# A decoder layer with experts on one core: scores from three bfloat16 parts in 64x64 tiles, normalizing on GpSimd, gelus that don't wait for the last exponentials, and first loads ordered by need

## The chip, the core and the metric

The kernel runs on one core of one Trainium2 chip. A core has five engines, each with an instruction queue of its own that it executes in order: TensorE (PE; its weight loads are listed apart as PEld), VectorE (DVE), ScalarE (ACT), GpSimd (POOL) and SyncE (SP). Transfers are issued from the queues of SyncE, ScalarE and GpSimd and carried by 16 DMA engines. Operands lie in SBUF, 128 partitions wide; TensorE writes PSUM, eight banks of 512 float32 a partition. The metric is the device time of one execution in microseconds (us), lower is better. Before has three runs, and one execution was profiled.

## What is computed

One layer of a decoder on x (32, 128, 128) with a context of the same shape; D = 128, 16 heads of 8, 8 experts of 512, two experts a token. All inputs and outputs are float32.

```python
x = layernorm(x + attn(x, x, x, sa_..., causal=True), ln1_g, ln1_b)
x = layernorm(x + attn(x, ctx, ctx, ca_..., causal=False), ln2_g, ln2_b)
x = layernorm(x + moe(x, router_w, router_b, w1, b1, w2, b2), ln3_g, ln3_b)

def attn(...):   # scores = Q K^T / sqrt(8), softmax over keys, times V, times wo, + bo
def moe(x, ...): # softmax of x @ rw + rb, the top 2, softmax of those two;
                 # sum of their experts gelu(x @ w1[e] + b1[e]) @ w2[e] + b2[e]
```

## The kernel before

**Order.** The kernel describes its work as tasks, each with an engine, an estimated duration, a priority, tasks that it depends on and buffers that it holds. `Plan.run` simulates the engines with these durations and fixes one order; `Plan.emit` writes the instructions in that order, so each engine's queue is set by the plan. PSUM is one pool, `s_ps`, of four double banks: a half step of scores takes a double bank, other work single banks. Score tasks have their priority moved ahead by `AHEAD` = 10 steps.

**Items and steps.** The 32 sequences are 8 groups of 4. Each group has a self item ("s") and a cross item ("c"), worked in the order s0 s1 s2 c0 s3 c1 ... s7 c5 c6 c7. A self item has three score tiles (the causal mask removes a quarter): "lo", 0 and 1 for queries and 0, 1 and "hi" for keys; a cross item has four. There are 56 tiles. Each is done twice: once with the queries on the partitions (`scores_q`), from which VectorE takes the negated row maximum (line 963), and `NL` = 3 tiles later with the keys on the partitions (`scores_k`), with the transposed maxima added by matmuls with `sel` (`top_k`), from which ScalarE writes the exponentials `pr` (line 1359). Each tile has two half steps of 8 heads, so 112 half steps each way. `emit_step` merges the query half step of tile i with the key half step of tile i - 3 into one stream: float32 matmuls in 32x64 tiles of the array, the queries on one half of the rows and the keys on the other. Float32 matmuls appear as two instructions. The causal mask is added by matmuls with `idj`.

**Q and K.** `prepare` loads the input, transposes it, projects K and V, and for self items Q (`queries`). Weights are permuted so that four heads' queries can be spread over `qm` by four transfers (line 822), with zeros at other heads' rows:

```python
def masked():
    for r in range(4):
        nc.sync.dma_start(out=it.qm.at[r::4, r, :], in_=it.q.at[r::4, :])
```

**Values and what follows.** `self_values` and `cross_values` multiply `pr` with V and a column of ones; `normalized` transposes on VectorE, takes the reciprocals, multiplies (line 1069) and transposes back; `finish_self` and `cross_out` apply wo and the residual; `norm` is the layer norm (statistics on VectorE, a power on GpSimd, lines 1097 and 1098, scaling on ScalarE). The cross item's Q comes from `finish_self` of its group. `finish_cross` computes the routing (one exponential at line 1212, one at 1290), scatters each token's row twice to its expert's region `rows_d` with eight indirect transfers on GpSimd (line 1266), and writes x2 = normalized * g2 + b2 to SBUF on GpSimd (lines 1186 and 1187).

**Experts.** 71 blocks of 128 rows. Tables (`table`) tell each block's expert; the first 25 blocks need only five groups' routing, the rest all of it and eight fills (line 1560). A block loads its rows and w1 (SyncE), transposes (1606), multiplies by w1 (1624), takes gelu (1633), multiplies by w2 held in `wall` (1641), adds b2 (1654) and scatters its results on GpSimd (1659). Blocks start behind the last score step; a gelu depends on all exponentials:

```python
t = add("ACT", 1.2, pr0 + 0.5, gelu, [t, t_tab, t_b1c, *exps_all], [p1, h])
```

`final` loads a group's results, adds them to x2, normalizes, scales on GpSimd and stores.

**Start.** Weights, biases and constants are loaded by `load`, most of them in ScalarE's queue (line 474); the group inputs by SyncE.

Of the kernel before, what the change touches and what calls it, by code (L numbers as in the profile page):

```python
# [16 lines left out]
P = 128  # L17
H = 16
HD = 8
E = 8  # L20
# [19 lines left out]
CLOCK = 1.0  # L40

# [109 lines left out]
class Plan:  # L151
# [18 lines left out]
    def run(self):  # L170
# [7 lines left out]
        mode = None  # L178
        order, events, k = [], [], 0
# [6 lines left out]
        while left:  # L186
            for e in engines:
                while free[e] <= now + 1e-9 and ready[e]:
                    put, got = [], None
                    while ready[e]:  # L190
                        item = heapq.heappop(ready[e])
                        taken = []
                        ok = True
                        for b in item[2].bufs:
# [24 lines left out]
                    if t.mode is not None:  # L219
# [17 lines left out]
            if what is not None:  # L237
# [15 lines left out]
                else:  # L253
                    heapq.heappush(ready[t.eng], (t.prio, t.start, t))
# [36 lines left out]
def kernel(  # L291
# [66 lines left out]
    idj = sb([P, 2, HALF], "idj", BF16)  # L358
    sel = sb([P, 4, HALF], "sel", BF16)
    maskq = sb([P, 2, HALF], "maskq", BF16)  # L360
    maskk = sb([P, 2, HALF], "maskk", BF16)
# [32 lines left out]
    def c_rowi2():  # L394
        nc.vector.tensor_scalar(ti[:, 1:2], ti[:, 0:1], 31, None, ALU.bitwise_and)
        nc.vector.tensor_copy(rowi, ti[:, 1:2])
# [22 lines left out]
    def c_cols2():  # L419
# [4 lines left out]
        nc.vector.tensor_tensor(tf[:, 128:192], c, r, ALU.subtract)  # L424
        nc.vector.tensor_scalar(tf[:, 192:256], tf[:, 128:192], -32.0, None, ALU.add)
        d = tf[:, 128:256].rearrange("p (j c) -> p j c", j=2)
        nc.vector.tensor_scalar(idj, d, 0.0, None, ALU.is_equal)
# [5 lines left out]
    def c_sel():  # L433
        for r in range(4):
            nc.vector.tensor_scalar(tf[:, r : r + 1], rowi, float(r), None, ALU.is_equal)
            nc.vector.tensor_scalar(tf[:, 4 + r : 5 + r], rowi, float(4 + r), None, ALU.is_equal)
        nc.vector.tensor_tensor(tf[:, 8:12], tf[:, 0:4], tf[:, 4:8], ALU.add)
        nc.vector.tensor_copy(sel, bc(tf[:, 8:12], 2, HALF))

    t_sel = early("DVE", 2.0, -10, c_sel, [t_rowi])  # L440
# [31 lines left out]
    def load(dst, src, prio, q="ACTQ", deps=()):  # L472
        eng = nc.sync if q == "SP" else nc.scalar
        return add(q, 0.12, prio, lambda: eng.dma_start(out=dst, in_=src), deps, lat=DMA)
# [11 lines left out]
    for i, (n, w) in enumerate(  # L486
        (("wqs", sa_wq), ("wks", sa_wk), ("wvs", sa_wv), ("wkc", ca_wk),
         ("wvc", ca_wv), ("wos", sa_wo), ("wqc", ca_wq), ("woc", ca_wo))
    ):
        raw[n] = spare[:, P * i : P * i + P] if n in ("wqs", "wks", "wkc", "wqc") else sb([P, P], n)  # L490
        t_raw[n] = load(raw[n], w, -30 + i)

    bias4 = sb([4, P], "bias4")
    t_b4 = [
        load(bias4[i : i + 1, :], b.rearrange("(o n) -> o n", o=1), -29.9 + 0.01 * i)
        for i, b in enumerate((sa_bq, sa_bk, ca_bq, ca_bk))
    ]
    cols = {}
    t_col = {}
    for n, src in (("g1", ln1_g), ("b1", ln1_b), ("g2", ln2_g), ("b2", ln2_b), ("bvs", sa_bv), ("bvc", ca_bv)):  # L500
        cols[n] = sb([P, 1], "col_" + n)
        t_col[n] = load(cols[n], colsrc(src), -22)
    rws = {}
    t_row = {}
    for n, src, w in (
# [4 lines left out]
        t_row[n] = load(rws[n], rowsrc(src, w), -18 if n != "bos" else -23)  # L510
    rw = sb([P, E], "rw")
    t_rw = load(rw, router_w, -17)


    def permuted(ap):
        return ap.rearrange("p (g r d) -> p g d r", g=4, r=4)

    def as_gdr(ap):
        return ap.rearrange("p (g d r) -> p g d r", g=4, r=4)

    wp = {}
    t_wp = {}
    for i, n in enumerate(("wqs", "wks", "wkc")):
        wp[n] = sb([P, P], n + "p")
        t_wp[n] = early(
            "DVE", 0.3, -15 + i,
# [1225 lines left out]
```

## Time and profile before

| | |
|---|---|
| runs | 746.95, 738.94 and 747.14 us, median 746.95 |
| profiled execution | 744.84 us, of which the span of the trace is 743.1 |
| busy, us | PE 588.1, PEld 475.0, DVE 341.3, ACT 321.0, POOL 259.5 |
| granted TensorE clock, mean | 0.893 |
| DMA | 52.73 MB in 53012 packets, mean 71 GB/s |
| costliest groups | the row maxima, DVE line 963, 137.1 us; the exponentials, ACT line 1359, 114.4 us; score matmuls of 32x128, line 845, 173.8 us |

Times count from the span's start. A row of the timeline gives start, duration, engine, line, operation, and out<-in with partitions x elements; x16 is a count, and rows close together are merged. A row of a group gives busy us and the mean ns of one, then the idle time of the engine ahead of it and what ended it. In a row of windows each engine's busy us and (instruction count) stand in the order PE, PEld, DVE, ACT, POOL, then the clock granted to TensorE as a share, the busy share of the 16 DMA engines, and GB/s; where only some instructions are asked for, engines that have none are left out. Busy time of overlapping instructions counts once, and a matmul's end is modelled.

### The profile page before, as it was taken

How to read it: one execution, taken by the hardware profiler on the slowest of the kernel's cores; microseconds unless marked ns; L12 is line 12 of the kernel's file. 1: busy time of each engine (PE TensorE's matmuls, PEld its weight loads, DVE VectorE, ACT ScalarE, POOL GpSimd, SP SyncE). 2: the span in 40 equal slices, each digit the busy share in tenths (PEclk: the TensorE clock that was granted, in tenths of full speed). 3: DMA queues.
4: the chain of work that ended last, by engine and by line, in shares of the span. 5: the costliest groups of instructions: out<-in, count | busy, mean ns of one | idle time of the engine just before them, and what ended most of it. 6: DMA issues, size and time to landing. Idle time of an engine off the chain costs nothing.

```text
span 743.1 us, 31241 instructions
## 1 busy us (share of the span) xinstructions
PE 588.1 (79%) x12852; PEld 475.0 (64%) x12852; DVE 341.3 (46%) x1009; ACT 321.0 (43%) x717; POOL 259.5 (35%) x440
## 2 busy tenths in 40 slices
PE   1689888998989998998898847985469996877740
PEld 1367666676767776766677736675459985866740
DVE  4445345464665553665655634464022225523332
ACT  0403245454355254254254312544236664556630
POOL 5000011012162422252422063347744444475552
PEclk9957899999999899899999975998859997879985
DMA  6410011000020010010000003022845474555211
GB/s 154 126 36 19 4 41 36 19 24 25 19 70 15 31 41 28 7 60 16 31 21 6 4 29 89 24 63 79 273 113 168 135 218 141 179 154 174 76 52 42
DMA packets 53012, 52.73 MB, mean 71 GB/s; under 512 B 7759, under 2 KB 39415, under 8 KB 52872
## 3 DMA queue, kind: packets, MB, share of 16 engines
q1 hardware_dynamic: 44976, 40.74, 18.6%
q0 software_dynamic: 4576, 9.00, 3.6%
q8 instruction: 103, 1.69, 1.0%
q10 hardware_dynamic: 3320, 1.00, 0.8%
q14 instruction: 37, 0.30, 0.1%
HBM read 35.36 MB, written 11.61 MB: 63 GB/s over the span
## 4 chain that ended last, share of the span: by engine, by line
PE 62%; issue 10%; ACT 7%; DMA 7%; DVE 6%; POOL 3%; SPq 2%; ACTq 2%; DVEq 1%; POOLq 0%
PE ps L845 35%; PE ps L1624 6%; PE ps L1641 6%; PE ps L740 4%; ACT pr L1359 3%; DVE nm L963 2%; PE ps L1606 2%; ACT k L1633 2%; DMA xT<-rows_d 1%; ACT y L1111 1%; POOL rows_d L1266 1%; PE ps L734 1%; PE ps L781 1%; PE ps L1132 1%; DMA res_d<-o,id 1%
## 5 line engine op out<-in xcount | busy, mean ns | idle before, releaser
L963 DVE TENSOR_REDUCE nm<-ps 128x8 f32<-128x1024 f32 (+1 forms) x112 | 137.1, 1224 | 150.3 <-PE ps L845 139.6
L1359 ACT ACTIVATE pr<-ps 128x1024 f32<-128x1024 f32 x112 | 114.4, 1023 | 182.9 <-PE ps L845 170.5
L845 PE MATMUL ps<-k,qm 32*64 32x128 f32 (+1 forms) x4096 | 173.8, 284 | 7.1 <-DMA qm<-q 5.3
L845 PEld LDWEIGHTS ps<-k,qm 32*64 32x64 f32 x4096 | 133.8, 145 | 35.8 <-issue 27.9
L845 PE MATMUL ps<-qm,k 32*64 32x512 f32 (+1 forms) x1024 | 131.7, 590 | 16.2 <-ACT pr L1359 5.4
L1633 ACT ACTIVATE k<-ps,b1c 128x128 f32<-128x128 f32 x284 | 80.6, 372 | 58.5 <-PE ps L1624 49.6
L975 POOL CAST nmx<-nm 128x16 bf16<-128x16 f32 x64 | 12.9, 201 | 249.2 <-DVE nm L963 242.5
L1641 PE MATMUL ps<-wall,k 128*128 x568 | 82.5, 292 | 17.1 <-ACT k L1633 13.3
L1659 POOL DMA_INDIRECT res_d<-o,id x71 | 69.8, 983 | 60.0 <-DVE o L1654 47.7
L845 PE MATMUL ps<-pr,v 64*32 64x64 f32 (+2 forms) x3072 | 76.0, 271 | 14.2 <-issue 10.1
L1641 PEld LDWEIGHTS ps<-wall,k 128*128 128x128 f32 x568 | 72.3, 200 | 22.0 <-ACT k L1633 15.1
L845 PEld LDWEIGHTS ps<-pr,v 64*32 64x32 f32 (+1 forms) x3072 | 59.2, 112 | 26.1 <-issue 16.3
L1266 POOL DMA_INDIRECT rows_d<-y,rid x64 | 64.2, 1003 | 28.9 <-issue 17.3
L845 PEld LDWEIGHTS ps<-qm,k 32*64 32x64 f32 x1024 | 32.0, 135 | 37.1 <-ACT pr L1359 11.5
L1624 PE MATMUL ps<-bx,qm 128*128 128x128 f32 x368 | 55.5, 301 | 0.0
L1651 DVE TENSOR_SCALAR id<-xT,tab_e 128x1 int32<-128x1 f32 x47 | 12.8, 273 | 89.3 <-PE ps L1606 21.9
L845 PE MATMUL ps<-nmT,sel 32*64 32x128 bf16 x1792 | 52.4, 225 | 1.6 <-issue 1.6
L1624 PEld LDWEIGHTS ps<-bx,qm 128*128 128x128 f32 x368 | 51.3, 216 | 0.4 <-ACT bx L1611 0.3
L1611 ACT ACTIVATE bx<-ps,col_b,col_g 128x128 f32<-128x128 f32 x71 | 32.3, 468 | 30.8 <-PE ps L1606 30.5
L845 PEld LDWEIGHTS <-sel 32*64 32x64 bf16 x1792 | 39.6, 106 | 6.6 <-issue 6.1
L1606 PE MATMUL ps<-ident,xT 128*128 128x128 f32 x47 | 15.0, 319 | 24.2 <-DMA xT<-rows_d 18.6
L1111 ACT ACTIVATE y<-ps,rs 128x128 f32<-128x128 f32 x64 | 24.7, 460 | 16.9 <-DVE rs L1103 16.9
(263 smaller groups left out, 867.8 us busy)
## 6 DMA issues: line engine op xcount, KB each, us to landing
qm<-in_L_xattn_e_w_dram SPq DMA_DIRECT2D x46, 256.0 KB, 3.2
w<-in_L_xattn_e_w_dram SPq DMA_DIRECT2D x25, 256.0 KB, 2.9
qm<-q SPq DMA_DIRECT2D x64, 64.0 KB, 1.9
pr<-res_d SPq DMA_DIRECT2D x8, 512.0 KB
xT<-rows_d SPq DMA_DIRECT2D x47, 65.0 KB, 2.1
xin<-in_x_dram SPq DMA_DIRECT2D x8, 256.0 KB, 3.2
xin<-in_ctx_dram SPq DMA_DIRECT2D x8, 256.0 KB, 4.2
wall<-in_L_xattn_e_w_dram SPq DMA_DIRECT2D x8, 256.0 KB, 5.9
```

Source lines behind the costliest of these rows:

```text
L740: nc.tensor.matmul(bank, lhsT=w, rhs=xT.rearrange("p s t -> p (s t)"), start=True, stop=True)
L845: nc.tensor.matmul(out_, lhsT=lhsT, rhs=rhs, start=start, stop=stop, skip_group_check=True)
L963: lambda: nc.vector.tensor_reduce(dst(), src(), AX.X, ALU.max, negate=True), [dep], [pair, nm],
L1111: lambda i=i: nc.scalar.activation(dst(i), src(i), AF.Identity, bias=rs.at[:, 1, i : i + 1], scale=rs.at[:, 0, i : i + 1],),
L1266: nc.gpsimd.indirect_dma_start(out=rows_d[:, :], out_offset=bass.IndirectOffsetOnAxis(ap=rid.at[:, i, k : k + 1], axis=0), in_=y.at[:, i, ...
L1359: lambda kp=kp, prb=prb, kh=kh: nc.scalar.activation(prb.at[:, 8 * kh : 8 * kh + 8, :].rearrange("p h q -> p (h q)"), kp.at.rearrange("p b ...
L1606: nc.tensor.transpose(bt.at[:, 0:P], xr_()[:, 0:P], ident)
L1611: lambda: nc.scalar.activation(xT.at[:, 0:P], bt.at[:, 0:P], AF.Identity, bias=cols["b2"], scale=cols["g2"]),
L1624: nc.tensor.matmul(p1.at[:, c * P : (c + 1) * P], lhsT=w1.at[:, c, :], rhs=xT.at[:, 0:P], start=True, stop=True)
L1633: nc.scalar.activation(h.at[:, c, :], p1.at[:, c * P : (c + 1) * P], AF.Gelu, bias=b1c[:, bass.ds(r + c, 1)],)
L1641: nc.tensor.matmul(p2.at[:, 0:P], lhsT=h.at[:, c, :], rhs=flat[:, bass.ds(w["pe"] + c * P, P)], start=c == 0, stop=c == NFC - 1,)
L1659: nc.gpsimd.indirect_dma_start(out=res_d[:, :], out_offset=bass.IndirectOffsetOnAxis(ap=idb.at[:, 0:1], axis=0), in_=o.at, in_offset=None, ...
```

## The change

- **Scores.** Q and K are each cut into three bfloat16 parts. The projection is biased and rounded to the first part on ScalarE, the remainder is taken on VectorE, cast to the second part and subtracted to the third on GpSimd. The three go to DRAM in one transfer (`pd`), and six transfers gather them into `qk` [128, 8, 512] so that 64 rows hold one head's 8 dimensions times six products of parts and two rows of zeros. Scores are bfloat16 matmuls in 64x64 tiles, a query and a key task of their own instead of the merged step. At most two query and two key half steps are in flight (`TQ`, `TK`), a query tile waits for the keys of `LOCK` = 2 steps back, keys trail by `NL` = 2 tiles, and the loads of an item wait for the step 4 before it (`LEAD`). Weights are no longer permuted.
- **Normalizing.** The multiply of `normalized` moves from VectorE to GpSimd.
- **Gelus.** They no longer depend on the exponentials; the plan knows which table ScalarE holds and keeps gelus together. The routing's second exponential becomes a tanh in all groups, the first one in the last two.
- **x2** is written to DRAM and loaded again in `final`; the scaling on GpSimd comes behind the row scatters.
- **First loads.** The first input comes first, ScalarE's queue has four loads (wq, wk and their biases of self attention), everything else goes to SyncE by need.
- **Buffers.** Three `k` buffers where four were (only for h now), four `pr` for five, 12 late buffers for h of the rest blocks; estimated durations in the plan are changed.

The core of the diff:

```diff
+TABLE = 1.3
+BURST = 3
...
+                        if e == "ACT" and item[2].mode not in (None, table):
+                            same = any(u.mode == table for _, _, u in ready[e]) or any(u.mode == table for _, _, u in put)
+                            if same or (table == "exp" and exps and gelus < BURST):
+                                put.append(item)
+                                continue
...
-    qm_t = places(3, [P, 4, G * P], "qm")
+    qk_t = places(6, [P, 8, G * P], "qk", BF16)
+    s_p3 = Slots(places(2, [P, 3, G * P], "p3", BF16))
...
-    NL = 3
-    GATE = 4
+    NL = 2
+    LEAD = 4
+    TQ, TK, LOCK = 2, 2, 2
...
+    def parts(w, b, xT, deps, prio, terms, name):
+        bank, p3, r1, at = Buf(s_ps), Buf(s_p3), Buf(s_r1), Buf(s_qk)
+        pd = dram.tile([3, P, G * P], BF16, name="pd_" + name)
+        t1 = pe(1.12, prio, lambda: project(bank.at, w, xT.at), deps, [bank, xT, p3])
+        t2 = add(
             "ACT", act(512, 1), prio + 0.1,
+            lambda: nc.scalar.activation(p3.at[:, 0, :], bank.at, AF.Identity, bias=b), [t1], [bank, p3],
+        )
+        t3 = add(
+            "DVE", dve(512), prio + 0.2,
+            lambda: nc.vector.scalar_tensor_tensor(r1.at, bank.at, b, p3.at[:, 0, :], ALU.add, ALU.subtract),
+            [t2], [bank, p3, r1],
+        )
+        t4 = add("POOL", 0.8, prio + 0.3, lambda: nc.gpsimd.tensor_copy(p3.at[:, 1, :], r1.at), [t3], [p3, r1])
+        t5 = add(
+            "POOL", pool_tt(512), prio + 0.4,
+            lambda: nc.gpsimd.tensor_tensor(p3.at[:, 2, :], r1.at, p3.at[:, 1, :], ALU.subtract), [t4], [p3, r1],
+        )
+        t6 = add(
+            "SP", 0.5, prio + 0.5, lambda: nc.sync.dma_start(out=pd.rearrange("k p n -> p k n"), in_=p3.at), [t5], [p3], lat=2.2
+        )
+
+        def loads():
+            for t, k in enumerate(terms):
+                nc.sync.dma_start(
+                    out=at.at[t::8], in_=pd[k - 1].rearrange("(i a) n -> a i n", i=8)
+                )
+
+        t7 = add("SP", 3.0, prio + 0.6, loads, [t6, *t_qz[0 : 2 if name in ("qs0", "ks0") else 6]], [at], lat=3.0)
+        return at, t7, t5
...
+    def scores_q(sq, h, pair):
...
+        for r in range(4):
+            i = 4 * h + r
+            for n in range(len(cols_[0])):
+                for j in range(2):
+                    rr = slice(HALF * j, HALF * j + HALF)
+                    for ct in range(2):
+                        s, q0, k0, nk, c0 = cols_[ct][n]
+                        mm(pair[HALF * ct : HALF * ct + HALF, j, r * P + c0 : r * P + c0 + nk],
+                           Q[rr, i, s * P + q0 : s * P + q0 + HALF], K[rr, i, s * P + k0 : s * P + k0 + nk],
+                           r == 0 and n == 0, r == 3 and sq[0] == "c" and n == len(cols_[0]) - 1)
...
-            nc.vector.tensor_tensor(
+            nc.gpsimd.tensor_tensor(
                 u2.at.rearrange("p (b a j d) -> p a b j d", a=2, j=2, d=HD),
...
-        t_e = add("ACT", 0.25, prio + 1.1, lambda: nc.scalar.activation(v(96, 32), v(64, 32), AF.Exp), [t1], [rt])
+        late_ = gi >= NG - 2
+        t_e = add(
+            "ACT", 0.25, prio + 1.1,
+            lambda: nc.scalar.activation(v(96, 32), v(64, 32), AF.Tanh if late_ else AF.Exp, scale=0.5 if late_ else 1.0),
+            [t1], [rt], mode=None if late_ else "exp",
+        )
...
+            items[sq[0], sq[1]].t_Q.deps.append(step_tasks[i - LEAD])
+            items[sq[0], sq[1]].t_K.deps.append(step_tasks[i - LEAD])
...
-        t = add("ACT", 1.2, pr0 + 0.5, gelu, [t, t_tab, t_b1c, *exps_all], [p1, h])
+        t = add("ACT", 1.2, pr0 + 0.5, gelu, [t, t_tab, t_b1c], [p1, h], mode="gelu")
...
+        t_y = add(
+            "SP", 0.4, pr0 - 2, lambda: nc.sync.dma_start(out=y.at.rearrange("p s d -> p (s d)"), in_=x2_d[gi]),
+            [items["c", gi].t_x2, *exps_all], [y], lat=2.5,
+        )
```

More of the change, by code (lines that the diff above doesn't have):

```diff
@@ L178, in run @@
         mode = None
+        table, exps, gelus = "exp", sum(t.mode == "exp" for t in self.tasks), 0
         order, events, k = [], [], 0
@@ L218, in run @@
                     d = t.dur
-                    if t.mode is not None:
+                    if e == "ACT":
+                        exps -= t.mode == "exp"
+                        gelus -= t.mode == "gelu"
+                        if t.mode not in (None, table):
+                            table = t.mode
+                            d += TABLE
+                    elif t.mode is not None:
                         if mode is not None and t.mode != mode:
@@ L253, in run @@
                 else:
+                    gelus += t.mode == "gelu"
                     heapq.heappush(ready[t.eng], (t.prio, t.start, t))
@@ L433, in c_sel @@
     def c_sel():
[L434 to L440, printed above, removed]
+        c = tf[:, 64:72]
+        nc.vector.tensor_tensor(tf[:, 0:8], c, rowi.broadcast_to([P, 8]), ALU.is_equal)
+        nc.vector.tensor_scalar(tf[:, 8:16], c, 8.0, None, ALU.add)
+        nc.vector.tensor_tensor(tf[:, 8:16], tf[:, 8:16], rowi.broadcast_to([P, 8]), ALU.is_equal)
+        nc.vector.tensor_tensor(tf[:, 0:8], tf[:, 0:8], tf[:, 8:16], ALU.add)
+        nc.vector.tensor_copy(sel, bc(tf[:, 0:8], 2, HALF))
+    t_sel = early("DVE", 1.2, -10, c_sel, [t_rowi, t_cols])
     def c_misc():
@@ L596 @@
     )
-    x2 = [sb([P, G, P], f"x2_{g_}") for g_ in range(NG)]
-    b1r = sb([E * NFC, P], "b1r")
+    x2_d = [dram.tile([P, G * P], F32, name=f"x2_{g_}") for g_ in range(NG)]
+    b1r = spare[0 : E * NFC, P : 2 * P]
     b1c = sb([P, E * NFC], "b1c")
     b2r = sb([P, E, P], "b2r")
+    t_b1r = load(b1r, e_b1.rearrange("e (c f) -> (e c) f", f=P), 7, "SP")
+    bb = Buf(s_ps)
+    t = pe(0.2, 12, lambda bb=bb: nc.tensor.transpose(bb.at[:, 0 : E * NFC], b1r, ident[: E * NFC, : E * NFC]), [t_b1r, t_ident], [bb], "32x128")
+    t_b1c = add("DVE", 0.2, 12.1, lambda bb=bb: nc.vector.tensor_copy(b1c, bb.at[:, 0 : E * NFC]), [t], [bb])
     t_wall = []
@@ L683 @@
     t_qz = [
-        early("POOL" if i == 1 else "DVE", 1.3 if i != 1 else 1.9, -21 + 9 * i,
-              lambda i=i: (nc.gpsimd if i == 1 else nc.vector).memset(qm_t[i], 0.0))
-        for i in range(3)
-    ]
+        early("POOL" if i % 2 else "DVE", 1.8, -21 + 2 * i,
+              lambda i=i: (nc.gpsimd if i % 2 else nc.vector).memset(qk_t[i].bitcast(F32), 0.0))
+        for i in range(6)
+    ]
+    for q_, t in zip(s_qk.free, t_qz):
+        q_.last = [t]
     t_nz = early("POOL", 0.8, -12, lambda: [nc.gpsimd.memset(n, 0.0) for n in nmx_t])
@@ L943, in emit_step @@
[L943 to L954 removed]
+                        mm(pair[HALF * ct : HALF * ct + HALF, j, r * P + c0 : r * P + c0 + nq],
+                           K[rr, i, s * P + k0 : s * P + k0 + HALF], Q[rr, i, s * P + q0 : s * P + q0 + nq],
+                           r == 0 and n == 0, False)
@@ L1074, in mul @@
             )
-        t = add("DVE", dve(256), prio + 0.02, mul, [t], [u1, rc, u2])
+        t = add("POOL", pool_tt(256), prio + 0.02, mul, [t], [u1, rc, u2])
         t = add(
```

436 lines of the change are left out of this document (180 added, 256 removed).

## The prediction

> **What bounds the kernel now.** I read the busy times first, then the stages, then inside each stage what its first late engine waits for.
>
> ```profile
> PE 588.1 (79%) x12852; PEld 475.0 (64%) x12852; DVE 341.3 (46%) x1009; ACT 321.0 (43%) x717; POOL 259.5 (35%) x440
> ```
>
> TensorE is the busiest engine by far, but 79% is an average. The windows cut the span at the first score (38.7 us) and the last one (484.8 us); the columns are busy us of each engine, then the granted clock and the DMA share.
>
> ```profile
> 38.70:93.00 54.30, 48.33 (x1495) 38.59 (x1501) 23.77 (x32) 13.57 (x20) 4.01 (x20) 0.69 0.05 16
> 93.00:260.00 167.00, 152.22 (x4675) 115.57 (x4659) 92.53 (x210) 76.55 (x126) 40.30 (x94) 0.98 0.10 31
> 260.00:427.30 167.30, 151.03 (x4414) 116.55 (x4412) 96.78 (x246) 75.69 (x127) 46.87 (x107) 0.97 0.08 24
> 427.30:450.40 23.10, 11.79 (x90) 9.03 (x90) 8.13 (x41) 4.88 (x13) 13.28 (x15) 0.72 0.10 34
> 450.40:484.80 34.40, 31.33 (x750) 22.33 (x754) 17.85 (x45) 14.09 (x19) 11.29 (x25) 0.79 0.19 53
> sum 446.10, PE 394.70 PEld 302.07 DVE 239.07 ACT 184.79 POOL 115.75; mean PE 78.94 PEld 60.41 DVE 47.81 ACT 36.96 POOL 23.15
> ```
>
> So the attention stage takes 446.1 us, TensorE works 394.7 of them (91% from 93 to 427 us), and 51.4 are idle, 11.3 of these in the hole at 427 to 450 us. It is a TensorE stage. The next two rows are the same windows summed for line 845 alone (scores and values), and for the tile pr (values only).
>
> ```profile
> sum 446.10, PE 286.36 PEld 222.32; mean PE 57.27 PEld 44.46
> ...
> sum 446.10, PE 73.06 PEld 56.80 DVE 0.00 ACT 113.35; mean PE 14.61 PEld 11.36 DVE 0.00 ACT 22.67
> ```
>
> Scores take 286.4 - 73.1 = 213.3 us of TensorE, 1.90 us for each of 112 half steps. The 181.4 us beside them (394.7 - 213.3) stay. Ahead of this stage ScalarE starts late; behind it the experts' stage has its holes:
>
> ```profile
> 0.79 0.43 ACTq L474 DMA_DIRECT2D wall<-in_L_xattn_sa_wq_dram  x1
> ...
> 17.90 0.33 ACTq L474 DMA_DIRECT2D rw<-in_L_xattn_router_w_dram  x1
> 18.26 1.28 ACT L758 ACT_TABLE_LOAD   x1 [18.26 <-DMA row_g<-in_L_xattn_ln_g_dram]
> ```
> ```profile
> 484.80:508.00 23.20, 15.40 (x196) 13.71 (x193) 13.11 (x72) 10.17 (x24) 12.85 (x18) 0.96 0.26 87
> 508.00:530.00 22.00, 18.65 (x136) 17.17 (x136) 7.09 (x33) 12.36 (x44) 16.36 (x22) 0.89 0.42 121
> 530.00:544.70 14.70, 0.45 (x1) 0.18 (x1) 2.35 (x10) 0.46 (x1) 10.58 (x11) 0.61 0.75 248
> 544.70:613.00 68.30, 65.85 (x485) 60.51 (x485) 13.78 (x57) 43.13 (x144) 28.23 (x30) 0.93 0.58 163
> 613.00:725.00 112.00, 78.21 (x551) 72.12 (x551) 45.09 (x187) 59.76 (x189) 61.49 (x63) 0.86 0.44 129
> ```
>
> From 484.8 to 544.7 us TensorE idles 59.9 - 34.5 = 25.4 us; from 544.7 to 613 it is full.
>
> **The scores.** A half step of queries becomes 16 pairs of a weight load and a bfloat16 matmul (32 where a tile has two halves), one of keys the same, plus 16 pairs for the maxima; a masked half step adds 4 pairs. Over 112 half steps each way: 2048 + 2048 + 1792 + 384 = 6272 pairs, four at a time in the 64x64 tiles. The trace has no 64x64 score, but it has 16 pairs of bfloat16 with 128 columns, four at a time, whose successor begins right behind them:
>
> ```profile
> 480.92 0.40 PE L845 MATMUL ps<-nmT,sel 32*64 32x128 bf16 x16
> 480.92 0.24 PEld L845 LDWEIGHTS <-sel 32*64 32x64 bf16 x12 [0.30 <-issue]
> 481.25 0.30 PEld L1162 LDWEIGHTS ps<-woc,oT 128*128 128x128 f32 x2
> ```
>
> From 480.92 to 481.25 is 0.33 us for 16, or 20.6 ns a pair: 129 us in all. The 384 masks are two to four times as wide (16 us more at three times), 1024 pairs are half as wide (10 us less at half): 135 us. The first tenth runs at the clock of 0.69 seen above, for which I add 10 us: 145. TensorE gains 213 - 145 = 68 us. The bounds: the weight loads alone start every 12 ns or so ((0.24 us less one load of 0.106, a mean from the group below) / 11), which would give 75 us and a gain of 138; and at 34 ns (213.3 / 6272) nothing is gained. I take 20.6 because that row has the new type and width.
>
> ```profile
> L845 PEld LDWEIGHTS <-sel 32*64 32x64 bf16 x1792 | 39.6, 106 | 6.6 <-issue 6.1
> L845 PE MATMUL ps<-nmT,sel 32*64 32x128 bf16 x1792 | 52.4, 225 | 1.6 <-issue 1.6
> ```
>
> A rule speaks against this. The Trainium skill, "TensorEngine Tiling (Array Packing)", section "Key Properties", says that changing the tiling mode drains TensorE. The row just shown has its successor in another mode 0.33 us behind the first start, so one such drain is inside my 20.6 ns; no run here shows the 64x64 mode itself. Splitting each mixed step into a query and a key group makes 112 more boundaries; what they could cost is a rival below.
>
> **What the scores now need first.** Each of 32 projections (16 items, Q and K) is cut into three parts and goes through DRAM. These are the nearest rows:
>
> ```profile
> L771 ACT ACTIVATE k<-ps,bqk 128x512 f32<-128x512 f32 x16 | 11.0, 690 | 23.3 <-PE ps L740 23.3
> 419.39 0.68 DVE L1497 TENSOR_TENSOR u<-ps,key_first 128x512 f32<-128x512 f32 x1
> L1187 POOL TENSOR_TENSOR x<-x,row_b 128x512 f32<-128x512 f32 x8 | 10.2, 1271 | 0.6
> L822 SPq DMA_DIRECT2D qm<-q x64: 458/592/1868, 34.2 to 448.4; - x64
> DMA to landing us min/median/max: 1.8/1.9/3.9
> L1069 DVE TENSOR_TENSOR u<-u,rc 128x256 f32<-128x256 f32 x32 | 13.3, 427 | 0.4
> ```
>
> The ScalarE pass (0.69) stays. New are a VectorE difference of 0.68 us (the row reads PSUM at the same size), a GpSimd cast (no row; I take 0.85, between nothing and the 1.27 of a two-input pass) and a GpSimd difference of 1.27; then one store (0.59 to issue, 1.9 to land) and six loads (3.55, 1.9) where four transfers stood (2.37, 1.9). The way from projection to score grows from 4.3 to 10.7 us, up to 14.7 with both landings at 3.9. By engine: VectorE 239 + 32 x 0.68 - 32 x 0.43 (the multiply that leaves) = 247; GpSimd 116 + 32 x 2.12 + 32 x 0.64 (half of 1.27) = 204; SyncE issues 224 transfers for 132 us. None reaches TensorE's 181 + 145 = 326 us.
>
> The longer way is covered in mid-stage, where a cross item waits behind four other items' steps. It isn't at the end, in the hole from 427 us: there the last cross queries wait for a norm that stands behind eight scatters in GpSimd's queue,
>
> ```profile
> 428.55 1.12 POOL L1266 DMA_INDIRECT rows_d<-y,rid  x1 [1.76 <-DVE whi L1296]
> ...
> 439.18 1.04 POOL L1098 TENSOR_TENSOR rs<-rs,mhalf 128x4 f32<-128x4 f32 x1
> ```
>
> and the 6 to 10 us come on top; I count 8. Elsewhere idle grows because VectorE (247 us) is now close behind, and the split maxima (nmx) and norms wait behind longer GpSimd work. Two new limits, two query and two key groups in flight and queries held until the keys of two steps back are issued, put waits at the head of TensorE's queue, with values and projections behind them. Against that the keys trail by two tiles where they trailed by three. I count 11 more. So idle goes from 51 to 70, bounds 51 and its double. Attention: 326 + 70 = 396, **-50 us** (from -138 to about +50, were nothing gained and idle doubled).
>
> The multiply on GpSimd costs 0.64 for 0.43, 32 times, in chains that scores cover; for the last group it is 0.4 us on the path. TensorE keeps all its other work. The eight wall loads now wait for the transposed b1 too; wall is first read at 508 us. Fewer constants, unpermuted weights and one vector less in the routing are nothing beside these.
>
> **The start.** ScalarE issues 27 loads until 18.2 us and only then loads its table; the first score follows at 38.8.
>
> ```profile
> 0.80 3.44 DMA xin<-in_x_dram
> ...
> 20.99 5.46 PE ps L740 x8
> ...
> 38.81 3.86 PE ps L845 x124
> ```
>
>  Now it issues four (27 from 0.79 to 18.2 are 0.64 us each with their waits, 0.43 for one alone), and SyncE has the rest. After: input landed at 4.3, transposes and copy 6.5, both projections 10.7 (eight pieces took 5.46 with their waits, so four about 2.7 to 4), parts 14, store 17, 12 loads and landing 26; SyncE's own 30 or so loads (13 us at 0.43, 19 at 0.64) can stand ahead of the stores, so I take 28: **-11 us** (from -15 to 0).
>
> **The experts.** Gelus waited for the last routing exponential:
>
> ```profile
> 506.48 1.28 ACT L1633 ACT_TABLE_LOAD   x1 [0.47 <-DVE wlo L1295]
> 507.78 5.26 ACT L1633 ACTIVATE k<-ps,b1c 128x128 f32<-128x128 f32 x20
> 525.06 0.97 POOL L1560 DMA_INDIRECT rows_d<-fillrow,fid  x1 [0.30 <-issue]
> 535.27 0.97 POOL L1659 DMA_INDIRECT res_d<-o,id  x1 [0.30 <-issue]
> ```
>
> Freed, they can start behind the last score's exponential, some 20 us sooner. What is late next is GpSimd: its eight row scatters and eight fills stand ahead of the results' scatters (535.27), and with four result buffers the experts stop. So of 25.4 us idle I take 15: **-15 us**. Bounds: -25, and +8, since eight reloads of x2 join SyncE's queue and three h buffers stand where four did. The tanh in routing costs three VectorE instructions of about 0.17 us, twice, beside other work.
>
> **The sum.** 743.1 - 50 - 11 - 15 = 667.1 us span; the profiled run took 744.84, 1.7 more, so **669 us**. The runs' median is 746.95; 2% of it, 15 us, is what a measurement of this kernel can tell.
>
> **Rivals.**
> 1. *Boundaries* (0.06). Each of 112 new boundaries waits for the last matmul to leave: its 225 ns less the 82 that its tile takes a pair anyway (4 x 20.6), 0.14 us, 16 us: 685. For it: separate groups; against: the row at 481.25. This is what the skill's drain would do.
> 2. *Others pace* (0.14). VectorE's reduce sits in every half step, GpSimd doubles its work; idle doubles to 103 us. Attention 429: 702. For it: 247 us of VectorE in a stage of 396. Against: it waits for TensorE today.
> 3. *The clock falls* (0.06). The windows grant 0.69 to 0.79 where TensorE is broken up and 0.98 where it is 91% busy. With 82% busy it might average 0.75 for 0.91: 326 x 0.91 / 0.75 = 396 + idle 50: 446, so 719. The Trainium skill, "TensorE: Matmul & The Clock Gate", section "What's actually happening", has half rate after an idle window; the windows at 0.69 to 0.79 agree in kind.
> 4. *Slower: the round trip through SyncE* (0.07). An item's loads start four tile steps ahead, and SyncE executes in order, so a store that waits for GpSimd holds up every load behind it. By rows the pair of projections needs 14 x 0.59 + 2 x 1.9 + 4 = 16 us against four steps of 396 / 58 = 27. If small rows of 1 KB made it 37, an item (3.5 steps) would take 32.4: 16 x 32.4 = 518 for 446, so 790. It turns slower than now beyond 34 us. For it: DRAM and 16 partitions a load, no row; against: twice the slack.
> 5. *It does more* (0.10). Idle stays at 51, the hole shrinks, the experts gain all 25: 640 or less.
>
> The forecast keeps 0.57. Also possible: that tanh is not in the same table as exp or gelu, 1.28 us a switch; at most some 10 us in the transition, inside the range. Range: from 615 (rival 5, pairs nearer 15 ns) to 725 (rival 3). Faster by over 2% (below 730): 0.57 + 0.06 + 0.14 + 0.10 and half of 3, **0.90**; within 2% the other half, **0.03**; slower **0.07**.
>
> **What will show it.** Scores: a cross half step of queries near 0.33 us and of keys near 0.66; the stage from first to last score near 396, TensorE near 326 in it, VectorE near 247, GpSimd near 204. First score near 28 us. First gelu within 3 us of the last exponential; TensorE idle in the next 60 us nearer 10 than 25. Wrong if pairs cost 30 ns or more, if score matmuls wait for the loads of the parts, or if the clock in mid-stage is below 0.85.

## The result: 705 us where 669 were forecast, and the profile after

The changed kernel takes 705.23 us (median of four executions), against 743.63 us for the kernel before beside it: a ratio of 0.948, 95% interval [0.940, 0.957]. Three of the four lie between 704.14 and 705.83 us; one, with a granted clock of 0.63, took 745.16 us and is left out of the ratio. The direction was right. The size was not: the span fell by 40.7 us (743.1 to 702.4), where I had summed 76.

The first line of the profile after shows what a reader wants first: TensorE has 81 us less work, and is idle more.

```profile
PE 507.0 (72%) x11443; PEld 407.8 (58%) x11443; DVE 355.2 (51%) x996; ACT 319.3 (45%) x717; POOL 335.1 (48%) x538
```

The windows from the first score (33.8 us) to the last one (448.6 us) of the changed kernel, and then the sums of the same windows for line 845 alone (scores and values) and for the tile pr (values only):

```profile
33.80:93.00 59.20, 43.32 (x1590) 31.32 (x1589) 32.63 (x60) 22.16 (x33) 17.36 (x44) 0.87 0.44 132
93.00:260.00 167.00, 134.11 (x4265) 101.56 (x4267) 106.92 (x225) 83.86 (x140) 75.75 (x146) 0.96 0.42 127
260.00:402.10 142.10, 112.13 (x3627) 88.45 (x3614) 87.02 (x222) 66.37 (x112) 61.81 (x122) 0.94 0.31 96
402.10:422.60 20.50, 11.16 (x131) 9.03 (x124) 8.07 (x32) 5.08 (x9) 15.19 (x18) 0.75 0.31 98
422.60:448.60 26.00, 17.86 (x477) 14.39 (x476) 18.83 (x65) 9.47 (x19) 15.64 (x33) 0.67 0.28 78
sum 414.80, PE 318.59 PEld 244.76 DVE 253.47 ACT 186.94 POOL 185.76; mean PE 63.72 PEld 48.95 DVE 50.69 ACT 37.39 POOL 37.15
```
```profile
sum 414.80, PE 198.58 PEld 157.09; mean PE 39.72 PEld 31.42
...
sum 414.80, PE 71.46 PEld 55.10 DVE 0.00 ACT 108.02; mean PE 14.29 PEld 11.02 DVE 0.00 ACT 21.60
```

So 40.7 us have three sources. The start gave 5 (first score at 33.8 for 38.8). The attention stage gave 31 (446.1 to 414.8). Behind the last score 253.8 us are left for 258.3, which is 4.5. In the stage TensorE's work fell by 76 us (394.7 to 318.6), more than forecast, and its idle time rose by 45 (51.4 to 96.2). The views of TensorE's waits in that stretch say where; the columns are the total, the number of times and the longest one. Before, then after:

```profile
PE ps L845 <- issue: 14.1, 17, 1.7
...
PE ps L1162 <- DVE oT L1079: 1.7, 1, 1.7
```
```profile
PE ps L845 <- issue: 30.3, 25, 2.4
PE ps L1128 <- DVE oT L1045: 19.9, 5, 8.7
PE ps L845 <- DVE nm L923: 7.9, 9, 2.6
```

Two rows make 34 of the 45 us: "issue", a wait for nothing that the profile shows, and the cross output (line 1162 before, 1128 after) waiting for the transposed values. By the windows, the hole before the last cross item didn't grow (9.3 us idle from 402 to 422 us, 11.3 before); idle time grew in the windows around it. Behind the last score, the gelus do start early, as meant (5.0 us behind the last exponential, which ends at 450.4 us), and then something new appears; the rows are ScalarE's timeline, two windows, and TensorE's waits there:

```profile
454.07 1.28 ACT L1622 ACT_TABLE_LOAD   x1 [2.30 <-PE ps L1595]
455.36 1.14 ACT L1622 ACTIVATE k<-ps,b1c 128x128 f32<-128x128 f32 x4
```
```profile
448.60:508.70 60.10, 45.15 (x415) 40.21 (x404) 18.04 (x94) 31.94 (x97) 41.37 (x48) 1.00 0.61 175
508.70:577.00 68.30, 50.08 (x363) 44.69 (x363) 13.36 (x54) 31.74 (x106) 25.23 (x26) 0.90 0.52 154
```
```profile
PE ps L1613 <- ACT qk L1622: 12.9, 22, 0.7
PE ps L1613 <- ACT k L1622: 5.3, 8, 0.8
```

In the first 60 us TensorE idles 15.0 us where before it idled 25.4; but in the next 68 us it idles 18.2, where before it was full (2.5). The first matmul of a block (line 1613) waits 30 times for the gelu of the block ahead of it. One round, from the timeline:

```profile
541.72 1.16 PE L1613 MATMUL ps<-bx,qk 128*128 128x128 f32 x8 [0.66 <-ACT qk L1622]
...
543.35 1.14 ACT L1622 ACTIVATE qk<-ps,b1c 128x128 f32<-128x128 f32 x4 [1.33 <-PE ps L1613]
...
544.54 1.16 PE L1613 MATMUL ps<-bx,qk 128*128 128x128 f32 x8 [0.66 <-ACT qk L1622]
```

A block's first matmuls of 1.16 us, 0.47 until the gelu starts, 1.14 of gelu, and at once the next block's matmuls: a loop of 2.82 us through one PSUM bank. The block's output bank is the one that the previous gelu has just left. In the kernel before, the median distance of two blocks is 2.22 us.

### The profile page after: what moved, and what is told of

Its sections match the earlier page's. It is cut to its first block, busy times and chain, and to the rows that moved or that the text cites. A ratio compares the mean times of both kernels' runs of the same rounds, so it can differ in the third digit from the quotient of the medians.

```text
span 702.4 us, 28754 instructions
## 1 busy us (share of the span) xinstructions
PE 507.0 (72%) x11443; PEld 407.8 (58%) x11443; DVE 355.2 (51%) x996; ACT 319.3 (45%) x717; POOL 335.1 (48%) x538
## 4 chain that ended last, share of the span: by engine, by line
PE 33%; DVE 15%; issue 14%; DMA 11%; POOL 10%; ACT 8%; SPq 6%; ACTq 2%; DVEq 1%; POOLq 0%
PE ps L845 14%; PE ps L1613 6%; DVE nm L923 5%; POOL rows_d L1232 4%; SPq L819 4%; PE ps L1630 3%; ACT pr L1340 2%; ACT qk L1622 2%; DMA pd_qs<-p 2%; DVE y L1678 2%; DMA pr<-res_d 2%; PE ps L733 2%; ACT k L1622 1%; DVE st L1057 1%; DMA qk<-pd_ks 1%
## 5 line engine op out<-in xcount | busy, mean ns | idle before, releaser
L845 PE MATMUL ps<-qk,qk 64*64 64x128 bf16 (+1 forms) x4096 | 98.8, 226 | 27.5 <-DVE nm L923 7.9
L845 PEld LDWEIGHTS <-qk 64*64 64x64 bf16 x4096 | 70.3, 115 | 60.7 <-issue 28.4
L845 PE MATMUL ps<-pr,v 64*32 64x128 f32 (+2 forms) x3072 | 73.6, 265 | 20.4 <-issue 14.2
L1622 ACT ACTIVATE qk<-ps,b1c 128x128 f32<-128x128 f32 x184 | 52.4, 368 | 45.0 <-PE ps L1613 41.8
L1613 PE MATMUL ps<-bx,qk 128*128 128x128 f32 x368 | 54.6, 295 | 17.6 <-ACT qk L1622 12.9
L1613 PEld LDWEIGHTS ps<-bx,qk 128*128 128x128 f32 x368 | 47.7, 203 | 24.0 <-ACT qk L1622 18.2
L845 PE MATMUL ps<-nmT,sel 64*64 64x128 bf16 x1792 | 49.7, 227 | 7.0 <-issue 6.6
L1630 PE MATMUL ps<-wall,qk 128*128 x368 | 50.2, 282 | 5.1 <-ACT qk L1622 2.3
L1630 PEld LDWEIGHTS ps<-wall,qk 128*128 128x128 f32 x368 | 45.4, 195 | 6.7 <-ACT qk L1622 3.3
L1622 ACT ACTIVATE k<-ps,b1c 128x128 f32<-128x128 f32 x100 | 28.6, 369 | 30.7 <-PE ps L1613 23.6
L1600 ACT ACTIVATE bx<-ps,col_b,col_g 128x128 f32<-128x128 f32 x71 | 32.6, 470 | 20.6 <-PE ps L1595 19.7
```

Of the source, the lines that this page charges most:

```text
L845: nc.tensor.matmul(out_, lhsT=lhsT, rhs=rhs, start=start, stop=stop, skip_group_check=True)
L1600: lambda: nc.scalar.activation(xT.at[:, 0:P], bt.at[:, 0:P], AF.Identity, bias=cols["b2"], scale=cols["g2"]),
L1613: nc.tensor.matmul(p1.at[:, c * P : (c + 1) * P], lhsT=w1.at[:, c, :], rhs=xT.at[:, 0:P], start=True, stop=True)
L1622: nc.scalar.activation(h.at[:, c, :], p1.at[:, c * P : (c + 1) * P], AF.Gelu, bias=b1c[:, bass.ds(r + c, 1)],)
L1630: nc.tensor.matmul(p2.at[:, 0:P], lhsT=h.at[:, c, :], rhs=flat[:, bass.ds(w["pe"] + c * P, P)], start=c == 0, stop=c == NFC - 1,)
```

## The experiments

They ran on three other chips, on which the kernel before takes 824 to 830 us with a clock of about 0.85; so ratios are compared, or times on these chips, which differ by some us for one kernel. The times expected below were reckoned for the first chip; run again on one of these, the changed kernel itself has a ratio of 0.933, not 0.948, and its edits have to be set against that. My theory after the comparison: **(a)** the gelus earned their 15 us, and the planner's new durations took them back through the reuse of a bank; **(b)** in attention "issue" is TensorE waiting for its own instructions; **(c)** the cross output waits because the multiply stands in GpSimd's queue. The rivals: VectorE and GpSimd pace the stage, as in the prediction's second rival, and what follows the gelus sets the end anyway.

**Banks.** For the experts' blocks the planner takes the half bank given back longest ago:

```diff
+        if n == 0:
+            free = [(self.given.get((i, h), 0), -i, h) for i, u in enumerate(self.used) for h in range(2) if not u[h]]
...
+            _, i, h = min(free)
```

> The changed kernel with one edit in the planner: the experts' blocks take the PSUM half bank that was given back longest ago, not the one given back last. Theory (bank reuse): the new estimated durations let the plan give the next block's first matmul the bank that the previous block's gelu has just left, so TensorE waits for ScalarE's gelu in 30 blocks, 18.2 us in all (12.9 + 5.3). With other banks these waits fall below 4 us, the pitch of a block in the long stretch from 2.82 to about 2.2 us, and the kernel takes 705 - 15 = 690 us (684 to 697). Rival (the gelu's own chain paces the blocks: 0.47 us to start, 1.14 to run, then the copy of the next rows): the waits get another name, the pitch stays at 2.8 us, and the time stays within 3 us of 705.

Measured: 750.14 us, ratio 0.907 [0.899, 0.916]. TensorE no longer waits for a gelu at the first matmul, and the median distance of blocks is 2.27 us. Its second matmuls in the long stretch come 2.0 us apart:

```profile
599.95 1.07 PE L1640 MATMUL ps<-wall,qk 128*128 x8
602.07 1.06 PE L1640 MATMUL ps<-wall,qk 128*128 x8
603.97 1.09 PE L1640 MATMUL ps<-wall,qk 128*128 x8
```

Theory (a) holds: from the last score to the end are 266.4 us. It is also the fastest version of this study that computes the whole layer. Run again on another chip:

> The kernel with the experts' banks given in turn once more, as the measure for the two beside it. Theory: ratio to the kernel before 0.907 as measured (0.895 to 0.92), 264 to 268 us behind the last score. Rival (the first reading was a disturbed one): 0.93 or more.

Measured: 751.73 us, ratio 0.913 [0.903, 0.922], 266.0 us behind the last score. The changed kernel itself, for comparison:

> The changed kernel as it is, as the measure for the edits run beside it on the same chip, since chips differ in their granted clock. Theory (the gelus earned their 15 us and the reuse of a PSUM bank took them back): its ratio to the kernel before is 0.948, as measured first, equal to that of the gated kernel (0.949) within 0.012 only if gating also hides the reuse; I expect 0.93 to 0.95, its stage from first to last score on a chip of the same clock within 5 us of those of the three edits before (445 to 449 us), and the time behind the last score within 5 us of the 284.7 us of the kernel with the multiply on VectorE. Rival (the rotation of banks did something else): the time behind the last score is below 275 us here too.

Measured: 770.2 us, ratio 0.933 [0.923, 0.943]; 280.1 us behind the last score, 4.6 less than the kernel with the multiply on VectorE, as the theory had it. The stage took 455.8 us, 7 to 11 more than the edits before it, so it missed that part; kernels with one order of instructions differ by up to 10 us in this stage from chip to chip. Behind the last score the banks are worth 14 us against this kernel.

**Gating.** The gelus wait for all exponentials and the routing again; the edit also takes them out of the planner's rule about tables:

```diff
-        t = add("ACT", 1.2, pr0 + 0.5, gelu, [t, t_tab, t_b1c], [p1, h], mode="gelu")
+        t = add("ACT", 1.2, pr0 + 0.5, gelu, [t, t_tab, t_b1c, *exps_all], [p1, h])
+        exps_all.append(t_e2)
```

> The changed kernel with the gelus waiting again for the last score exponential and for the routing's second function of all groups (which stays a tanh), without the planner's table rule. This undoes the part that the prediction put at -15 us. If freeing the gelus is worth that, this kernel takes 720 us (714 to 728), with the first gelu some 25 us behind the last exponential instead of 5. Rival (what follows, GpSimd's scatters and the fills, sets the experts' end either way): 703 to 709.

Measured: 782.27 us, ratio 0.949 [0.942, 0.956]. The last score is at 478.2 us, and ScalarE loads the gelu's table 34 us later:

```profile
512.27 1.28 ACT L1623 ACT_TABLE_LOAD   x1 [0.46 <-DVE rt L1220]
513.57 3.20 ACT L1623 ACTIVATE k<-ps,b1c 128x128 f32<-128x128 f32 x12
```

Behind the last score 300.3 us are left, 16 to 20 more than in the two ungated kernels with the old banks (284.7 and 280.1). And with both edits:

> Both edits together: banks given in turn, and the gelus gated again by the exponentials and the routing. It completes the square of gating and banks. Theory (two separate effects, gelus freed 15 us, banks 16 to 18): the time behind the last score is that of the kernel with the banks alone plus 15 us (280 to 286), ratio about 0.927. Rival (the reuse of banks matters only because the gelus are spread; gated gelus run in bursts in another order): gating costs less than 5 us here.

Measured: 765.23 us, ratio 0.922 [0.910, 0.933]; 280.9 us behind the last score, 15 more than the banks alone. The square is complete: freeing the gelus is worth 15 to 20 us whichever banks are used, the reuse of banks costs 14 to 19 whether they are gated or not. The rival falls.

**The multiply.** Back on VectorE:

```diff
-            nc.gpsimd.tensor_tensor(
+            nc.vector.tensor_tensor(
...
-        t = add("POOL", pool_tt(256), prio + 0.02, mul, [t], [u1, rc, u2])
+        t = add("DVE", dve(256), prio + 0.02, mul, [t], [u1, rc, u2])
```

> The changed kernel with the multiply of the normalizing put back on VectorE. Theory (a queue behind GpSimd): TensorE's waits of the cross output for the transposed values (21.4 us in all, 8.7 of them in the hole at 407 us) come from the multiply standing in GpSimd's queue behind scatters, casts and the maxima's split; they fall below 9 us and the kernel takes 694 us (687 to 701). Rival (VectorE paces the stage, as in the prediction's second rival): 32 multiplies of 0.43 us more on VectorE make the maxima later; the wait for the output shrinks but TensorE waits longer for the maxima, and the time is 703 to 712.

Measured: 769.54 us, ratio 0.936 [0.927, 0.944]. That would be the theory's 694 us on the first chip, but the changed kernel itself has 0.933 on such a chip, so nothing is gained. The wait of the cross output falls from 6.6 us (in the banks' kernel on the same chip) to 1.9, and the stage doesn't shorten. Its window, and that of the banks' kernel on the same chip:

```profile
33.20:481.60 448.40, 342.49 (x10054) 255.08 (x10057) 255.89 (x608) 185.69 (x308) 167.78 (x324) 0.84 0.34 105
```
```profile
33.10:480.60 447.50, 339.99 (x10048) 254.43 (x10047) 250.39 (x602) 187.26 (x310) 186.17 (x361) 0.87 0.34 105
```

So the multiply has no price on this chip, but only one such wait stood there, 6.6 us in the hole. On the first chip there were five, 19.9 us, and its trace shows the queue that theory (c) named. At each of the five the multiply (line 1035) ran behind the group's eight scatters (line 1232), as here:

```profile
295.53 0.35 DVE L1027 RECIPROCAL rc<-u 128x32 f32<-128x32 f32 x1
296.37 0.97 POOL L1232 DMA_INDIRECT rows_d<-y,rid  x1 [0.30 <-issue]
300.97 0.61 POOL L1035 TENSOR_TENSOR u<-u,rc 128x256 f32<-128x256 f32 x1
302.12 0.79 PE L1128 MATMUL ps<-woc,oT 128*128 128x128 f32 x2 [3.27 <-DVE oT L1045]
```

Its operand was there at 295.88 us, the last scatter ended at 297.34, a norm and parts came next, and the multiply started at 300.97. What this costs the stage on the first chip was not measured.

**TensorE or the others?** Two edits that leave every queue's order as it is, and leave out work. One takes 1344 pairs from TensorE, the other 57 us from VectorE:

```diff
-        for r in range(4):
+        for r in (3,):
```

> The changed kernel with the row maxima subtracted for one of each four heads only: 12 of the 16 pairs with sel leave each key half step, 1344 pairs in all, every queue otherwise in the same order. (It leaves out the subtraction for the other heads.) Theory (TensorE with its instruction blocks still sets most of the stage): 1344 pairs at 20.3 ns are 27 us of work, and 10.5 blocks of instructions at 3.5 us or more need not be fetched, so the stalls at blocks (36 us) fall by 8 to 15: the stage shortens by 30 us (24 to 42). Rival (the others pace it, as in the prediction's second rival): the freed time turns into waits for VectorE and GpSimd, and the stage shortens by less than 12 us.

```diff
-            src = lambda: pair.at.rearrange("p b (r k) -> p (b r) k", r=4)
+            src = lambda: pair.at.rearrange("p b (r k) -> p (b r) k", r=4)[:, :, 0:HALF]
```

> The changed kernel with each row maximum taken over the first half of its columns, all queues in the same order. (It leaves out the other half of the columns.) A reduce takes about 0.69 us for 1.22, 59 us less of VectorE's 253 in the stage. Theory (TensorE and its instruction blocks): only the 5 to 8 us of waits for a maximum go, the stage shortens by 3 to 10 us. Rival (VectorE paces the stage, the prediction's second rival): it shortens by 25 us or more.

Measured: 741.32 us, ratio 0.896 [0.885, 0.908], and 762.29 us, ratio 0.926 [0.916, 0.936]. The stage's windows of the unedited kernel, of fewer maxima and of the half reduce, all on one chip:

```profile
34.10:489.90 455.80, 341.10 (x10047) 255.77 (x10047) 249.94 (x601) 186.36 (x308) 185.88 (x360) 0.86 0.34 104
```
```profile
33.40:453.80 420.40, 317.68 (x8704) 230.35 (x8703) 248.67 (x602) 185.51 (x309) 186.49 (x360) 0.86 0.36 111
```
```profile
33.10:474.70 441.60, 336.38 (x10048) 256.74 (x10047) 192.92 (x602) 186.62 (x310) 186.12 (x361) 0.86 0.34 106
```

Fewer pairs shorten the stage by 35.4 us (24 to 42 expected), 12 more than TensorE's busy time falls (23.4); TensorE's idle time falls too. (Set against the same order on the other two chips, 447.5 and 446.4 us, it is 26 to 27.) Taking 57 us from VectorE shortens it by 14.2, or by 5 to 6 when set against the other two chips, somewhere between the bounds of the two theories, but far from 57. TensorE still sets most of this stage, and VectorE a little of it.

**The instructions.** A series of independent pairs with nothing else:

> Not the decoder: only series of independent bfloat16 matmuls in 64x64 tiles of TensorE, four tiles in turn, 1152 pairs of a weight load and a matmul with 64 columns, 1152 with 128, 768 with 256, and again 1152 with 128 beside transfers of the kind that gather the parts. Theory (instruction stream): 16 KB blocks of instructions, 256 instructions or 128 pairs each, arrive no faster than one in 3.4 to 3.7 us, so long series of 64 and of 128 columns both take 27 to 29 ns a pair, with stalls of 1 to 2 us at every block, while 256 columns take about 45 ns without stalls; the transfers change this by less than 10%. Rival (the stalls in the kernel come from the transfers of the parts beside them): 128 columns take 20 to 22 ns a pair without stalls, and only the last series has them. Second rival (the stalls come from waits on other engines that the trace doesn't name): no stalls in any series.

TensorE's timeline in the series of 64 columns and of 128; x128 is the number of matmuls in one burst. Then the windows of the series of 64, 128 and 256 columns, and of 128 beside the transfers:

```profile
13.41 1.92 PE L365 MATMUL n<-wide 64*64 64x64 bf16 x128 [4.74 <-issue]
16.86 1.92 PE L365 MATMUL n<-wide 64*64 64x64 bf16 x128 [1.53 <-issue]
...
45.86 1.98 PE L365 MATMUL n<-wide 64*64 64x128 bf16 x128 [1.47 <-issue]
49.59 1.98 PE L365 MATMUL n<-wide 64*64 64x128 bf16 x128 [1.75 <-issue]
```
```profile
13.41:38.68 25.27, 13.45 (x896) 12.51 (x896) 0.00 (x0) 0.00 (x0) 1.00 0.02 5
45.86:70.87 25.01, 13.87 (x898) 12.85 (x897) 0.00 (x0) 0.00 (x0) 1.00 0.02 5
81.06:96.37 15.31, 15.26 (x546) 14.86 (x548) 0.00 (x0) 0.00 (x0) 1.00 0.02 6
98.88:130.08 31.20, 15.85 (x1024) 14.68 (x1024) 0.00 (x0) 0.00 (x0) 1.00 0.52 162
```

This is the clearest picture of the study. With 64 and 128 columns TensorE runs exactly 128 pairs in 1.92 to 1.98 us, 15 ns a pair, and then stands still until 3.45 to 4 us have passed since the burst began. Sustained, a pair costs 28 ns with 64 columns (25.27 / 896) and with 128 (25.01 / 898). With 256 it costs 28 ns too (15.31 / 546), where I had expected 45; there TensorE is busy all the time, 3.6 us for 128 pairs, and no stall shows. Beside the transfers it is 30.5 (31.20 / 1024), 9% more. The queue for instructions in the decoder's own profile has the size that belongs to it:

```profile
q8 instruction: 92, 1.51, 0.9%
```

That is 16.4 KB a packet, and 2 x 11443 instructions in 92 packets, some 249 in each. The decoder's own traces settle it, for they hold the time of each packet and of each instruction. In the changed kernel all 25 waits of the row "issue" at line 845 end 1.22 to 1.59 us behind the arrival of such a packet, and all stand at one place, give or take one, in a count of TensorE's instructions by 256. So do 16 of the 17 in the kernel before. Theory (b) holds, for the whole of that row on the first chip. It also explains the edit of the maxima: in the unedited kernel beside it 27 waits at this place take 30.2 us, with fewer pairs 13 take 12.6.

**The start**, with the first keys' store and loads in ScalarE's queue, and the banks:

```diff
+        q, eng = ("ACT", nc.scalar) if name == "ks0" else ("SP", nc.sync)
```

> The changed kernel with the banks given in turn as before, and with the first item's keys stored and gathered from ScalarE's queue beside SyncE's, so that twelve loads in one queue (7.7 us) become six in each of two. Theory (the start is set by the parts' way through one queue): the first score comes at 30 us for 33 (29 to 31.5), the banks take 18 us off behind the last score, together 0.905 of the time before (0.895 to 0.915). Rival (the start waits for the landing or for the projections ahead in TensorE's queue): the first score stays at 32.5 to 34 us and only the banks count.

Measured: 770.57 us, ratio 0.933 [0.926, 0.941]: a miss. The banks gave their part (264.1 us behind the last score), but the first score came at 35.4 us and the stage took 469.1. The keys' store was issued at 19.24 us, later than in SyncE's queue of the unedited kernel on that chip (18.43), behind copies of other items that wait for their inputs. The edit also changes the plan's order, and the stage was some 13 us longer than in that kernel; which part of the order did it stays open.

**The planner's durations**, set to what the traces show:

```diff
-        return 0.33 + (0 if sq[0] == "c" else 0.22 if sq[2] == "lo" else 0.11)
+        return 0.43 + (0 if sq[0] == "c" else 0.22 if sq[2] == "lo" else 0.11)
...
-        t7 = add("SP", 3.0, prio + 0.6, loads, [t6, *t_qz[0 : 2 if name in ("qs0", "ks0") else 6]], [at], lat=3.0)
+        t7 = add("SP", 3.86, prio + 0.6, loads, [t6, *t_qz[0 : 2 if name in ("qs0", "ks0") else 6]], [at], lat=3.0)
...
```

> Banks given in turn, and the plan told what the traces show: a query half step 0.43 us for 0.33 and a key half step 0.86 for 0.55 (16 and 32 pairs at 27 ns), six loads of parts 3.86 for 3.0, a scatter 1.28 for 1.1, the cast 0.62 for 0.8. Theory (the idle time at the head of TensorE's queue comes from an order made with too short times): 5 to 15 us fewer in the stage from first to last score, ratio 0.89 to 0.90. Rival (those times don't matter; the order scatters by some 10 us whatever the plan believes, as the edit of the start showed): within 10 us of the banks alone on either side.

Measured: 773.78 us, ratio 0.937 [0.929, 0.944]: neither, 22 us more than the banks alone. The stage took 453.5 us, but the first score came at 44.8 and 280.4 us were left behind the last one. Truer durations made a worse order here: in such a planner they also decide what goes first.

## Why the prediction was right, and where it fell short

The direction and the range (615 to 725) held. The sum of 667.1 us missed the span by 35: 26 too little for idle time in attention, 10.5 at the experts, 6 at the start, and 7 too much for TensorE's work.

**The scores** were under-promised. They take 127.1 us (198.6 - 71.5) for the forecast 145; with masks and narrow pairs in it, that is 20.3 ns a pair over 6272 pairs, for 23.1 forecast. TensorE's 318.6 us in the stage stand for 326. The row at 481.25 chose well, but it held more than a pair's pace. Here are two groups of maxima, the first followed by scores in the same 64x64 tiles, the second by values in 64x32 tiles:

```profile
167.47 0.39 PE L845 MATMUL ps<-nmT,sel 64*64 64x128 bf16 x16
167.69 0.39 PE L845 MATMUL ps<-qk,qk 64*64 64x128 bf16 x16
167.92 0.39 PE L845 MATMUL ps<-nmT,sel 64*64 64x128 bf16 x16
168.24 0.42 PE L845 MATMUL ps<-pr,v 64*32 64x128 f32 x6
```

From the start of 16 such pairs to the start of the next group are 0.224 us where that keeps the tiles (median of 57 in the stage), 14 ns a pair, and 0.324 where it changes them (median of 34); groups of 16 scores have 0.247 and 0.350. So a change of tiles costs 0.10 us, and the 20.6 ns of the forecast had one in every 16 pairs. That the mean came out near it is partly luck: pairs are faster, and masks, changes of tiles and the lower clock of some windows make up for it. The Trainium skill, "TensorEngine Tiling (Array Packing)", section "Key Properties", says that changing the tiling mode drains TensorE; the trace agrees, with these 0.10 us. The first rival had the price (0.14) nearly right and the count wrong: a query group and a key group share their tiles, and the stage has 271 such changes for 237 before, 34 more and not 112, which is 3.4 us. The third rival is out, since the stage's clock hardly fell (0.96 and 0.94 in the two long windows for 0.98 and 0.97); its premise was not in the rows either, for in the windows of 0.69 and 0.79 TensorE is 89% and 91% busy. So is the fourth (scores waited 3.0 us for the loads of the self keys and 1.6 for those of the cross queries).

**The idle time** is the step that failed: "idle goes from 51 to 70" became 96.2. Of the 19 us added, 8 were for the hole, which did not grow; elsewhere 11 were forecast and 47 came. That 96.2 is close to the 103 of the second rival, and its 702 us to the time measured, is luck. Its stage of 429 us was too long by 14, its start and experts too short by 16, and the mechanism shown is another. VectorE is busy 253 us (247 forecast) and GpSimd 186 (204), and the reduces alone set 5 to 14 us on the later chips.

The term that I had not seen is the stream of instructions. The stall was in the rows of before (14.1 us of "issue" at line 845), the forecast has no term for it, and denser pairs doubled it: 30.3. My bound from the weight loads (12 ns a pair) looked at the array, not at what feeds it. A pair runs in 15 ns and is delivered in 28. The other large row, 19.9 us at the cross output for 1.7, comes from the multiply, which the forecast priced at 0.4 us, "in chains that scores cover", and which stood behind eight scatters. 8.7 of it lie in the hole, where TensorE waited 7.0 for a norm before. What that row costs by itself, and how the rest of the 45 us splits between VectorE, GpSimd and the order of the plan, stays open.

**The start** gave 5 of 11. Parts ended at 15.5 us (14 forecast), the loads' landing was reckoned at 26 and came after 31 (the fourth of the keys' six loads at 31.2):

```profile
16.29 0.38 SPq L814 DMA_DIRECT2D pd_qs<-p  x1
...
17.92 0.38 SPq L814 DMA_DIRECT2D pd_ks<-p  x1
...
21.21 3.86 SPq L819 DMA_DIRECT2D qk<-pd_qs  x6
25.11 3.81 SPq L819 DMA_DIRECT2D qk<-pd_ks  x6
...
31.58 2.04 PE L733 MATMUL ps<-xT,wks 128*128 128x512 f32 x2 [1.61 <-issue]
...
33.80 0.65 PE L845 MATMUL ps<-qk,qk 64*64 64x64 bf16 x32
```

The mis-sized term is the landing: stores and loads of parts take 2.4 to 4.9 us in the median for the 1.9 I took from transfers of the old kind. And the next item's projection stood in TensorE's queue ahead of the first score, from 31.58 to 33.62.

**The experts** gave 4.5 of 15, and here the step was right and a step was missing. Gelus begin 6.8 us behind the last score (23.2 before), idle time in the next 60 us is 15.0 ("nearer 10 than 25"), and gating costs 15 to 20 us when put back. What I priced at nothing was the last words of the diff, the changed estimated durations. In the old plan a block's gelu is reckoned to end 0.03 us after the next block's first matmul begins, so that takes another bank; with TensorE's times some 10% longer in the plan, the gelu ends 0.10 us before, its bank is free, and the next matmul takes it and must wait for the real gelu, which starts 0.47 us late. In the plan of the kernel before, a block's first matmul takes the bank that the previous gelu has just left in 2 of 70 cases, in that of the changed kernel in 34, and in the changed plan with the old durations of a block's TensorE steps in 1. So it is these durations; no run was made with that edit.

**The tanh** cost no switch. The Trainium skill, "ScalarE: Activation LUTs", section "Table sets: the hidden batching unit", has tanh in the set of exp; the trace agrees, with two table loads in the whole kernel (2.70 and 454.07 us). A tanh also runs at 476.70 us, behind the gelus' load, without another: the gelu's set holds it too here.

## What to carry to other kernels

Ask of a stream of short matmuls not only what the array takes, but whether their instructions arrive: 256 in some 3.5 us here. A row "issue" in the middle of a group of matmuls is the sign, if it comes back every 256 instructions, and wider or fewer matmuls are the cure. In a kernel whose order and buffers come from a planner, a changed estimate is an edit like any other: look at which buffer the next user gets, and hand out the one free for longest. A small instruction moved to another engine waits for that engine's whole queue, so price it by what stands ahead of it. And when a wait vanishes and the stage stays, look at what sets the stage before moving more work.

## What the runs showed of the hardware that was not expected

The pace of TensorE's instructions above: 128 pairs at 15 ns, one such block in 3.45 us at best, alike for 64 and 128 columns; with 256 columns the pairs themselves take as long. And the change of tiles: 0.10 us each, in the decoder on every chip it ran on.

On the three later chips, in every decoder kernel, TensorE crawls in the attention stage while GpSimd issues a group's eight scatters. The windows are such 10 us of the unedited kernel on one of them, and on the first chip:

```profile
301.60:311.70 10.10, 3.81 (x81) 2.02 (x80) 2.22 (x8) 0.86 (x3) 7.96 (x9) 0.87 0.15 49
```
```profile
287.30:297.40 10.10, 8.82 (x294) 7.14 (x296) 5.57 (x12) 5.31 (x9) 7.96 (x9) 1.00 0.26 74
```

81 matmuls for 294, from 304 us on in bursts of one to five with 0.4 to 1.2 us between them, called "issue" again: it makes that row 61.1 us there for 30.3. These waits do not keep to the place in 256 instructions: 30.2 of the 61.1 us do, and the other 30.8 fall in or just behind the scatters. To see whether scatters alone do it:

> Not the decoder: 640 pairs of bfloat16 matmuls with 512 columns in 64x64 tiles, then 960 more of them while GpSimd issues eight scatters of 128 rows of 520 bytes. In the four decoder kernels on the second and third chip TensorE issued 67 to 81 matmuls in the 10 us of a group's scatters in attention, and 185 to 289 on the first chip. Theory (the scatters themselves hold up TensorE on these chips): beside the scatters the pairs slow to under half their rate. Rival (it is something else of the decoder at that time): the pairs keep their pace of about 57 ns within 10%.

```profile
30.00:44.00 14.00, 14.00 (x264) 7.27 (x260) 0.82 (x2) 0.85 (x1) 1.00 0.01 2
44.00:70.00 26.00, 26.00 (x488) 13.52 (x484) 0.00 (x0) 7.02 (x8) 1.00 0.07 23
```

They don't: 53 ns a pair with them (26.00 / 488) and without (14.00 / 264). There the eight scatters come 3.0 to 3.8 us apart, in the decoder 1.28; whether that matters, or the chip, stays open.
